# Denominators of the softmax from 32 rows ahead of v, and a range test of them for the bound on scores

## The chip, the cores and the metric

The kernel runs on one core of one Trainium2 chip. The metric is the device time of one execution in microseconds (us). Engines are named as in the profile: PE multiplies matrices, DVE, ACT and POOL work on vectors, SP issues most of the DMAs.

## The reference

Two layers on x of 8 images, 512 channels and 32 x 32 = 1024 positions, all in float32:

```python
# layer 0: attention over the positions, 8 heads of 64 channels
q, k, v = conv1x1(x, Wq, bq), conv1x1(x, Wk, bk), conv1x1(x, Wv, bv)
attn = softmax(einsum('bhdn,bhdm->bhnm', q, k) * 64 ** -0.5, axis=-1)
x = x + conv1x1(einsum('bhnm,bhdm->bhdn', attn, v).reshape(B, C, H, W), Wp, bp)
# layer 1: non-local block with 256 inner channels, then batch norm
theta, phi, g = (conv1x1(x, w, b).reshape(b, 256, n) for ...)
f = einsum('bcn,bdn->bcd', theta, phi) / n
z = conv1x1(einsum('bcd,bdn->bcn', f, g), W_w, W_b) + x
out = (z - mean) * rsqrt(var + 1e-5) * gamma + beta    # over batch and positions
```

## The kernel before

**Work of one image.** The kernel goes through the images b one by one: attention of b, then q, v and k of image b + 1, then the projection of b, its theta and phi, and the rest of the non-local block. The z of the last three images is finished late, in `last_z`, which also takes the batch norm's statistics, normalises and writes the output.

**Products.** Each 1x1 convolution is a product of 2 x 2 blocks, made by `seven` (L263) with seven block products in place of eight (Strassen's way, in Winograd's form); for q, k and the projection of most images some of the seven are again split so, by `nested` (L245). The sums of weight blocks that this needs are made once, on DVE (`weight_sums` L103, `keep_inner` L163), and kept in DRAM; `load_w` (L124) brings a kept set, up to 2.4 MB, back into a pool of two places. A set is issued on SP's queue when the product that used its place is done. The block products land in PSUM banks, of which there are four; ACT or DVE moves or adds them to the result (`first`, `add`), and a bank is used again when its reader is done. In v (`values` L408) the order of block products is 11, s1t1, s2t2, s4, s3t3, 12, t4, with eight matmuls (called units here, numbered from 0) each; the adds of v are at L418.

**Attention** (L436). For each pair of heads p and half of the queries h, PE makes scores for eight blocks of 128 keys (L462), ACT takes the exponential without a shift (L465), and DVE adds the eight results to `acc` (L469, L471), so that what is left for the denominator is a sum over 128 rows for each of two heads. `spread` (L503) brings each `acc` to `fold`: `together` (L498) writes the first quarter of its rows by a DMA of SP and adds the other three by accumulating DMAs of POOL, to 32 rows. When four are there, a second `together` (L524) adds the two halves of every pair of rows to 16.

**Denominators and normalisation.** `all_denominators` (L526) sums over the 16 rows by two matmuls with a matrix of ones and zeros (`folds8`), 64 columns wide, takes the reciprocal (L534, 128 x 512), writes 16 rows of it to DRAM (`den_d`, 32 KB, L536) and `rows_of` (L553) reads them back four times, each read spread over 64 partitions (`r`, 512 KB each, in 8 KB per partition, L558). `products` (L567) multiplies o by r in four DVE operations (L571). In the loop, `norm` does all but the products after v's block product 1 (that is, on PE between units 15 and 16), and the products follow v's block product 5. The last image has its own way (`denominators` L540), 128 x 512 at a time for half of the heads.

**Bound on the scores.** Because there is no shift, the kernel tests that the exponentials can't overflow: `peak_of` (L396) takes the largest |q| and |k| of every channel (64 reductions on DVE), `bound_scores` (L421) multiplies them, sums over the channels of a head by a small matmul with `heads`, compares with a bound, and multiplies q by the 0 or 1 that results (on POOL, L429). At the end of the program the smallest gate is counted by a matmul, read into a register, and the other program, `shifted`, is run if a test failed.

**What sets the order.** `pe`, `dve` and `sp` keep the instructions that are passed to them in the order of the program on PE, DVE and SP. All matmuls are pinned so; of the DVE's work, v's adds, the products o<-o,r, most of q's adds and data sums are, k's adds are not. The other instructions are placed by a scheduler when the kernel is built. SP issues DMAs in its order, and each waits at the head of its queue for what it needs. The `fold` pool has one place, used by `fold` and by `r` in turn.

## Time and profile before

| | us |
|---|---|
| three runs | 2145.25, 2145.33, 2148.92 |
| median | 2145.33 |
| span of the profiled execution | 2143.6 |
| period of one image (343.55 to 606.52) | 262.97 |
| PE busy in it | 262.85 |
| matmul of 512 columns, 128 x 128 | about 0.43 each |
| matmul of 256 columns, 128 x 128 | about 0.22 each |
| w_WkT load of 2368 KB, from issue to landing (median) | 8.8 |
| den_d store of 32 KB | 1.8 |
| r loads, 512 KB each (median) | 6.9 |
| last matmul | 2123.1 |

The profile is one execution. Its span runs from the first to the last instruction; the profiled execution's own time lies outside the page, and the median of the runs is 1.7 us above this span. Busy times of an engine are sums of its instructions; matmuls overlap at their edges by about 0.17 us, so a group's time is a little longer than the step to the next group. In a timeline each line is the start, the duration, the engine, the line of the kernel, the operation with what it writes and reads, the shape and the number of instructions; brackets give the idle time ahead of it and what ended it. SPq is SP's DMA queue: the duration there is that of issuing, not of the transfer.

### The profile page before, as it was taken

The numbers are of one execution on the slowest core, as the hardware profiler recorded it, in microseconds if no ns is written. First come the engines' busy times: TensorE is split into PE (matmuls) and PEld (weight loads), VectorE is DVE, ScalarE is ACT, GpSimd is POOL, SyncE is SP. The second block draws the span as 40 slices with busy tenths as digits, with TensorE's granted clock in tenths as the row PEclk, the third lists the DMA queues.
The fourth block names the chain that finished last, engine by engine and source line by source line (L and its number), as shares of the span: only waits on it lengthen the run. The fifth ranks groups of instructions, "written<-read, shape, count | busy, mean of one in ns | idle before, by whom it ended". The sixth has DMA issues, their size and how long they took to land.

```text
span 2143.6 us, 30444 instructions
## 1 busy us (share of the span) xinstructions
PE 2119.6 (99%) x12654; PEld 1123.3 (52%) x12654; DVE 1448.4 (68%) x1795; ACT 742.8 (35%) x848; POOL 193.2 (9%) x242
## 2 busy tenths in 40 slices
PE   9999999999999999999999999999999999999996
PEld 4534664356733567335673366633666347743462
DVE  6467667667676676766667667676675676756736
ACT  1464104641046310463105621066212652056106
POOL 0111000110001100011001100011000110011000
PEclk9999999999999999999999999999999999999998
DMA  6433443334143331433323342233434235122758
GB/s 242 137 46 58 136 166 127 49 71 129 73 131 49 79 116 73 133 50 83 109 102 109 48 100 99 97 107 50 108 132 161 42 45 139 52 60 39 227 197 341
DMA packets 53969, 231.05 MB, mean 108 GB/s; under 512 B 9792, under 2 KB 16192, under 8 KB 46272
## 3 DMA queue, kind: packets, MB, share of 16 engines
q1 hardware_dynamic: 42144, 199.26, 27.5%
q0 software_dynamic: 10192, 28.46, 11.0%
q8 instruction: 101, 1.65, 0.3%
q10 hardware_dynamic: 1488, 1.32, 0.2%
q14 instruction: 44, 0.36, 0.1%
HBM read 141.84 MB, written 46.27 MB: 88 GB/s over the span
## 4 chain that ended last, share of the span: by engine, by line
PE 96%; ACT 1%; DVE 1%; DMA 1%; issue 0%; SPq 0%; ACTq 0%; DVEq 0%
PE ps L462 21%; PE po L488 21%; PE pv L300 9%; PE ptp L300 9%; PE pp L300 7%; PE pk L300 6%; PE pq L300 5%; PE pg L300 4%; PE pk_in_s L255 3%; PE pq_in_s L255 3%; PE pz L300 2%; PE pf L658 2%; PE pp_in_s L255 2%; PE pwf L713 1%; ACT z L830 1%; PE pf L674 1%
## 5 line engine op out<-in xcount | busy, mean ns | idle before, releaser
L465 ACT ACTIVATE e<-ps 128x1024 f32<-128x1024 f32 x512 | 522.6, 1024 | 431.1 <-PE ps L462 425.6
L471 DVE TENSOR_TENSOR acc<-acc,e 128x1024 f32<-128x1024 f32 x384 | 470.0, 1224 | 143.7 <-ACT e L465 140.3
L462 PE MATMUL ps<-q,k 64*64 64x512 f32 x4096 | 529.4, 589 | 0.0
L488 PE MATMUL po<-e,v 64*64 64x512 f32 x4096 | 528.7, 589 | 0.0
L488 PEld LDWEIGHTS po<-e,v 64*64 64x64 f32 x4096 | 156.6, 133 | 282.9 <-issue 275.4
L462 PEld LDWEIGHTS ps<-q,k 64*64 64x64 f32 x4096 | 155.5, 133 | 283.8 <-issue 274.8
L501 POOL DMA_DIRECT2D fold<-acc x189 | 147.1, 779 | 978.9 <-DMA fold<-acc 576.6
L701 ACT ACTIVATE g<-pg,gb 128x512 f32<-128x512 f32 x31 | 21.3, 687 | 475.4 <-PE pg L300 475.3
L469 DVE TENSOR_TENSOR acc<-e,e 128x1024 f32<-128x1024 f32 x64 | 78.3, 1224 | 136.6 <-ACT e L465 136.6
L300 PE MATMUL pv<-w_WvT,t_x 128*128 128x256 f32 x512 | 116.4, 381 | 0.0
L300 PE MATMUL ptp<-w_tp,t_x 128*128 128x256 f32 x512 | 114.4, 379 | 0.0
L417 ACT COPY v<-pv 128x1024 f32<-128x1024 f32 x32 | 32.4, 1012 | 213.9 <-PE pv L300 213.9
L300 PEld LDWEIGHTS pv<-w_WvT,t_x 128*128 128x128 f32 x512 | 96.6, 190 | 18.5 <-issue 5.7
L300 PEld LDWEIGHTS ptp<-w_tp,t_x 128*128 128x128 f32 x512 | 97.3, 190 | 13.2
L300 PE MATMUL pq<-t_x,w_WqT 128*128 128x512 f32 x200 | 100.1, 592 | 0.8 <-DVE t_x L842 0.8
L300 PE MATMUL pp<-t_o,w_WpT 128*128 128x512 f32 x208 | 100.8, 592 | 0.0
L300 PE MATMUL pk<-t_x,w_WkT 128*128 128x512 f32 x200 | 100.0, 592 | 0.0
L429 POOL TENSOR_SCALAR q<-q,gates 128x1024 f32<-128x1024 f32 x32 | 35.1, 1109 | 718.4 <-DVE gates L427 718.4
L300 PE MATMUL ptp<-w_tp,x 128*128 128x256 f32 x384 | 87.4, 381 | 0.0
L300 PE MATMUL pv<-w_WvT,x 128*128 128x256 f32 x384 | 86.8, 379 | 0.0
L324 DVE TENSOR_TENSOR q<-q,pq_in_s 128x256 f32<-128x256 f32 x119 | 48.6, 420 | 51.1 <-PE pq_in_s L255 38.4
L324 DVE TENSOR_TENSOR k<-k,pk_in_s 128x256 f32<-128x256 f32 x119 | 47.9, 420 | 48.6 <-PE pk_in_s L255 36.0
(195 smaller groups left out, 2348.6 us busy)
## 6 DMA issues: line engine op xcount, KB each, us to landing
fold<-acc POOLq DMA_DIRECT2D x189, 128.0 KB, 3.1
w_WqT<-kept_WqT SPq DMA_DIRECT2D x7, 2368.0 KB, 8.8
w_WkT<-kept_WkT SPq DMA_DIRECT2D x7, 2368.0 KB, 8.8
r<-den_d SPq DMA_DIRECT2D x32, 512.0 KB, 6.9
x<-in_x_dram SPq DMA_DIRECT2D x30, 512.0 KB, 5.7
w_WpT<-kept_WpT SPq DMA_DIRECT2D x6, 2176.0 KB, 8.3
w_WvT<-kept_WvT SPq DMA_DIRECT2D x7, 1792.0 KB, 7.2
w_tp<-kept_tp SPq DMA_DIRECT2D x7, 1792.0 KB, 7.3
```

The costliest lines, as they stand in the source:

```text
L255: pe(nc.tensor.matmul(ps, a[wi], d[di], start=s not in begun, stop=True, skip_group_check=True))
L300: pe(nc.tensor.matmul(to_ps, lhsT(k), rhs(k), start=(s, at) not in begun, stop=(k == nk - 1), skip_group_check=True))
L324: pin(nc.vector.tensor_tensor(at, at, ps if len(ps.shape) == 3 else ps.unsqueeze(1), ALU.add))
L417: seven(f"pv_{b}", w, data, True, lambda q, ps: nc.scalar.copy(at(q), as_v(ps)), lambda q, ps: dve(nc.vector.tensor_tensor(at(q), at(q), a ...
L429: nc.gpsimd.tensor_scalar(q[:, p, :], q[:, p, :], gate[:, p:p + 1], 1.0, ALU.mult, ALU.mult)
L462: pe(nc.tensor.matmul(ps[c * P // 2:(c + 1) * P // 2, j, :], k[r, p, keys], q[r, p, h * 512:(h + 1) * 512], start=True, stop=True, skip_gr ...
L465: nc.scalar.activation(e, ps, AF.Exp, scale=SCALE)
L469: nc.vector.tensor_tensor(accs[u], es[u, 0], e, ALU.add)
L471: ins = nc.vector.tensor_tensor(accs[u], accs[u], e, ALU.add)
L488: pe(nc.tensor.matmul(ps[j * D:(j + 1) * D, r, :], v[keys, m, (2 * p + j) * D:(2 * p + j + 1) * D], e[keys, j, :], start=(m == 0), stop=(m ...
L501: nc.gpsimd.dma_start(to, part_of, accum_op=ALU.add)
L658: pe(nc.tensor.matmul(to, theta[l][:, i, :], phi[r][:, i, :], start=(i == 0), stop=(i == NB // 2 - 1), skip_group_check=True))
```

## The change

Four things are changed.

1. The test of the scores' bound goes: `peak_of`, `bound_scores`, the gates. In its place the reciprocals themselves are tested to lie between 1e-20 and 1e20: nine small loads bring them from DRAM into `dens` (128 x 512), and at the end two DVE operations compare, four transposes on PE and one reduction on DVE bring the result to one number per partition, which is counted as before.
2. The second folding goes. The denominators are summed from 32 rows by eight matmuls, 32 columns wide and 256 long, in four column tiles with two accumulating into each; the reciprocal is 128 x 256, `den_d` is [32, 256], and `r` is read in two pieces of 4 KB per partition, where it was one of 8 KB.
3. `den` moves from v to q's unit 14 (of 16), in a bank that q has finished with, and the four products o<-o,r from after v's block product 5 to v's units 32, 35, 38 and 41, each by itself. The reciprocal is pinned.
4. For image 0 the sums of WkT are pinned and come ahead of the inner sums and the store of WqT; the adds of every k are pinned.

Some code comes with it that these sizes do not use (`positions_out` in `nested`). In the order that is built, den_d, the four r and `dens` stand behind the load of w_WkT on SP's queue; before, they stood behind it as well, but were issued after v's block product 1.

```diff
-    def bound_scores(b, q, k, peak_q, peak_k):
-
-        nc.vector.tensor_tensor(peak_q, peak_q, peak_k, ALU.mult)
-        ps = next_bank(f"bound_{b}")[:, 0, :]
-        pe(nc.tensor.matmul(ps[:, :CC], heads, peak_q, start=True, stop=True))
...
-            if i == 3 and not make_f:
-                two = t[:, g, :].rearrange("(r s) n -> s r n", s=2)
-                together(t[g * D:(g + 1) * D, 2, :], [two[0], two[1]])
...
-            t, ps = t[:, 2, :], ps[:, 0, :]
-            columns(ps, folds8, lambda j: t[:, j * 512:(j + 1) * 512])
-            ri = t[:, :512]
-            nc.vector.reciprocal(ri, ps)
-            d = dram2.tile([16, 512], F32, tag="den", name=f"den_d_{b}")
-            nc.sync.dma_start(d, ri.rearrange("(a s) n -> a s n", a=16)[:, 0, :])
-            d = d.rearrange("(j g i) n -> g j (i n)", j=2, g=2)
-            return d[0], d[1]
+            ps, of = ps[:, 0, :256], P // 4
+            for g in range(2):
+                for i in range(4):
+                    pe(nc.tensor.matmul(ps[i * of:(i + 1) * of, :], folds4[:, g * of:(g + 1) * of],
+                                        t[:, g, i * 256:(i + 1) * 256], start=(g == 0), stop=(g == 1),
+                                        skip_group_check=True))
+            ri = t[:, 2, :256]
+            dve(nc.vector.reciprocal(ri, ps))
+            d = dram.tile([of, 256], F32, tag=f"den{b}", name=f"den_d_{b}")
+            nc.sync.dma_start(d, ri.rearrange("(x s) n -> x s n", s=4)[:, 0, :])
+            own.append((dens[:, b * 64:(b + 1) * 64], d.rearrange("x (y n) -> (x y) n", y=4)))
+            return d.rearrange("(j h g i) m -> g j h i m", j=2, h=2, g=2)
...
+                to = rows[g][j * D:(j + 1) * D, :]
+                if len(d.shape) == 4:
+                    to = to.rearrange("q (h n) -> q h n", h=2)
+                    sp(nc.sync.dma_start(to, d[j].rearrange("h i m -> h (i m)").partition_broadcast(D)))
...
-    q, peak_q = heads_of(0, "q", weights("WqT", True), bq, data, early=True, by_chunk=True)
-    keep_inner("WqT", w_first)
-    load_w(nc.sync)
+    q = heads_of(0, "q", weights("WqT", True), bq, data, dve, early=True, by_chunk=True)
...
-    w = weights("WkT")
-    k, peak_k = heads_of(0, "k", w, bk, data)
+    w = weights("WkT", pin=dve)
+    keep_inner("WqT", w_first)
+    load_w(nc.sync)
+    k = heads_of(0, "k", w, bk, data, dve)
...
+                     14: lambda: nxt.update(products=normalize(denominators(bank(free[0], f"den_{b}"))))}
+            q = heads_of(b + 1, "q", weights("WqT"), bq, nxt["data"], dve, inner="WqT", fills=fills)
             load_w(nc.sync)
-            def norm():
-                nxt["products"] = normalize(denominators(next_bank(f"den_{b}")))
-
-            v = values(b + 1, weights("WvT"), nxt["data"], {1: norm, 2: lambda: [one() for one in later], 5: lambda: nxt["products"]()})
+            free[:] = [free[2], free[1], free[0], free[3]]
+            v = values(b + 1, weights("WvT"), nxt["data"],
+                       fills={unit: lambda i=i: nxt["products"][i]() for i, unit in enumerate((32, 35, 38, 41))})
...
+    for to, d in own:
+        nc.sync.dma_start(to, d)
     last_z()
...
+    nc.vector.tensor_scalar(sane, dens, 1.0 / SANE, 1.0, ALU.is_ge, ALU.mult)
+    nc.vector.scalar_tensor_tensor(sane, dens, SANE, sane, ALU.is_le, ALU.mult)
+    ps = next_bank("sane_t")[:, 0, :]
+    for i in range(512 // P):
+        pe(nc.tensor.transpose(ps[:, i * P:(i + 1) * P], sane[:, i * P:(i + 1) * P], ident))
+    nc.vector.tensor_reduce(good, ps, AX.X, ALU.min)
```

More of the change, by code (lines that the diff above doesn't have):

```diff
@@ L19 @@
 EPS = 1e-5
-BOUND = 60.0
+SANE = 1e20
 def attention_nonlocal_kernel(tc: tile.TileContext, a: dict, out: bass.AP):
@@ L140, in load_w, with weights @@
             dma.dma_start(to, quarter(name, m, k))
-    def weights(name, sums_done=False):
+    def weights(name, sums_done=False, pin=lambda ins: None):
         n, w = loaded.pop(0)
@@ L147, in weights @@
             if not sums_done:
-                weight_sums(w, corner[name])
+                weight_sums(w, corner[name], pin=pin)
             if name not in ("WqT", "WkT"):
@@ L168, in keep_inner @@
                                  (s4, a12, s2, ALU.subtract)):
-                nc.vector.tensor_tensor(to, l, r, op)
+                dve(nc.vector.tensor_tensor(to, l, r, op))
         wide = len(INNER[name]) * 3 * P
@@ L243, in unshifted, with nested @@
              15: ((0, "22", False), (0, "21", False))}
-    def nested(name, stage, w, data, tags, first, add):
+    def nested(name, stage, w, data, tags, first, add, positions_out=False):
         slots = [bank(tag, f"{name}_in_{tag}") for tag in tags]
@@ L254, in nested @@
                 ps = pair[s % 2 if s < 2 else 1][:, s // 2, n % 2 * 256:(n % 2 + 1) * 256]
-                pe(nc.tensor.matmul(ps, a[wi], d[di], start=s not in begun, stop=True, skip_group_check=True))
+                if positions_out:
+                    ps = ps.rearrange("p (i f) -> p i f", f=P)
+                    for i in range(2):
+                        pe(nc.tensor.matmul(ps[:, i, :], d[di][:, i * P:(i + 1) * P], a[wi], start=s not in begun and not i,
+                                            stop=True, skip_group_check=True))
+                else:
+                    pe(nc.tensor.matmul(ps, a[wi], d[di], start=s not in begun, stop=True, skip_group_check=True))
                 begun.add(s)
                 for to, is_first in reads:
+                    if positions_out:
+                        (first if is_first and begins else add)((q, int(to[0]) - 1, int(to[1]) - 1), ps)
+                        continue
                     c = rows(q).start + int(to[0]) - 1
@@ L275, in seven @@
             free[:] = [tags[1], tags[2], tags[3], tags[0]]
-            steps = nested(name, inner, w, data, tags[2:], first, add)
+            steps = nested(name, inner, w, data, tags[2:], first, add, positions_out)
         def read(reads, ps):
@@ L295, in seven @@
                          for m in range(half // P)]
-            work = [(*part, k) for part in (parts if m is None else parts[m:m + 1]) for k in range(nk)]
+            each = len(parts) // 2
+            work = [(*part, k) for part in (parts if m is None else parts[m * each:(m + 1) * each]) for k in range(nk)]
             if by_chunk and what in ("11", "s1t1"):
                 work.sort(key=lambda one: one[4])
-            for to_ps, at, lhsT, rhs, k in work:
+            for i, (to_ps, at, lhsT, rhs, k) in enumerate(work):
                 pe(nc.tensor.matmul(to_ps, lhsT(k), rhs(k), start=(s, at) not in begun, stop=(k == nk - 1),
@@ L302, in seven @@
                 begun.add((s, at))
+                if three and positions_out and not i % 2:
+                    continue
                 for ahead in (True, False):
@@ L328, in unshifted @@
     xt = xp.tile([P, CC, N], F32, tag="x", name="x_0")
-    heads = const.tile([P, P], F32, tag="heads", name="heads")
-    nc.vector.memset(heads, 0.0)
+    zeros = w3.tile([P, N], F32, tag="acc", name="zeros")[:, :P]
+    nc.vector.memset(zeros, 0.0)
     _, w_first = weights_tile("WqT", C // 2)
@@ L344, in unshifted @@
     for i in range(WARM):
-        pe(nc.tensor.matmul(ps[:, :P], heads, heads, start=True, stop=True))
+        pe(nc.tensor.matmul(ps[:, :P], zeros, zeros, start=True, stop=True))
     bq, bk = load_col("bq", nc.scalar), load_col("bk", nc.scalar)
@@ L357, in unshifted @@
         nc.vector.memset(folds[i * P // 4:(i + 1) * P // 4, i * D // 4:(i + 1) * D // 4], 1.0)
-    folds8 = const.tile([P, D], F32, tag="folds8", name="folds8")
-    nc.gpsimd.memset(folds8, 0.0)
-    nc.gpsimd.affine_select(out=folds8, in_=folds8, compare_op=ALU.is_gt, fill=1.0, base=1 - P // 8,
-                            pattern=[[-P // 8, 8], [0, D // 8]], channel_multiplier=1)
-    nc.gpsimd.affine_select(out=folds8, in_=folds8, compare_op=ALU.is_ge, fill=0.0, base=0,
-                            pattern=[[-P // 8, 8], [0, D // 8]], channel_multiplier=1)
-    for j in range(2):
-        nc.vector.memset(heads[j * D:(j + 1) * D, j * D:(j + 1) * D], 1.0)
+    folds4 = const.tile([P, D], F32, tag="folds4", name="folds4")
+    nc.vector.memset(folds4, 0.0)
+    for i in range(4):
+        for at in (i * 4, P // 4 + 16 + i * 4):
+            nc.vector.memset(folds4[i * P // 4:(i + 1) * P // 4, at:at + 4], 1.0)
     mv = const.tile([P, CC, 2], F32, tag="mv", name="mv")
-    gates = const.tile([P, B * NPAIR], F32, tag="gates", name="gates")
+    dens = const.tile([P, B * HEADS * N // P], F32, tag="dens", name="dens")
     ngamma = const.tile([P, CC], F32, tag="ngamma", name="ngamma")
@@ L374, in halves, with heads_of @@
         return t.rearrange("p (h n) -> p h n", h=NH)
-    def heads_of(b, what, w, bias, data, pin=lambda ins: None, later=None, **how):
+    def heads_of(b, what, w, bias, data, pin=lambda ins: None, **how):
         t = mats.tile([P, CC, N], F32, tag=what, name=f"{what}_{b}")
-        peak = small.tile([P, CC], F32, tag=f"peak_{what}", name=f"peak_{what}_{b}")
         def first(q, ps):
@@ L394, in heads_of, with values @@
         seven(f"p{what}_{b}", w, data, False, first, add_to(t, pin), **how)
-        def peak_of(c):
-            ins = nc.vector.tensor_reduce(peak[:, c:c + 1], t[:, c, :], AX.X, ALU.max, apply_absolute_value=True)
-            if b == 0 or later is not None:
-                dve(ins)
-        for c in range(CC):
-            if later is None:
-                peak_of(c)
-            else:
-                later.append(lambda c=c: peak_of(c))
-        return t, peak
-    def values(b, w, data, between=None):
+        return t
+    def values(b, w, data, **how):
         v = mats.tile([P, NB, C], F32, tag="v", name=f"v_{b}")
         def at(q):
+            if isinstance(q, tuple):
+                q, o, n = q
+                n, o = (int(q[1]) - 1) * NB // 2 + n * 2, (int(q[0]) - 1) * C // 2 + o * P
+                return v[:, n:n + 2, o:o + P]
             return v[:, (int(q[1]) - 1) * NB // 2:int(q[1]) * NB // 2, (int(q[0]) - 1) * C // 2:int(q[0]) * C // 2]
         def as_v(ps):
-            return ps.rearrange("p h (i f) -> p (h i) f", f=C // 2)
+            return ps if ps.shape[2] == P else ps.rearrange("p h (i f) -> p (h i) f", f=C // 2)
         seven(f"pv_{b}", w, data, True, lambda q, ps: nc.scalar.copy(at(q), as_v(ps)),
-              lambda q, ps: dve(nc.vector.tensor_tensor(at(q), at(q), as_v(ps), ALU.add)), between)
+              lambda q, ps: dve(nc.vector.tensor_tensor(at(q), at(q), as_v(ps), ALU.add)), **how)
         return v
-    def bound_scores(b, q, k, peak_q, peak_k):
-        nc.vector.tensor_tensor(peak_q, peak_q, peak_k, ALU.mult)
-        ps = next_bank(f"bound_{b}")[:, 0, :]
-        pe(nc.tensor.matmul(ps[:, :CC], heads, peak_q, start=True, stop=True))
-        gate = gates[:, b * NPAIR:(b + 1) * NPAIR]
-        nc.vector.tensor_scalar(gate, ps[:, :CC], BOUND / SCALE, 1.0, ALU.is_le, ALU.mult)
-        for p in range(NPAIR):
-            nc.gpsimd.tensor_scalar(q[:, p, :], q[:, p, :], gate[:, p:p + 1], 1.0, ALU.mult, ALU.mult)
     def columns(ps, lhsT, rhs):
@@ L530, in all_denominators @@
                 bias_product(t[:, 3, :], ps[:, 1, :CC])
-            t, ps = t[:, 2, :], ps[:, 0, :]
-            columns(ps, folds8, lambda j: t[:, j * 512:(j + 1) * 512])
-            ri = t[:, :512]
-            nc.vector.reciprocal(ri, ps)
-            d = dram2.tile([16, 512], F32, tag="den", name=f"den_d_{b}")
-            nc.sync.dma_start(d, ri.rearrange("(a s) n -> a s n", a=16)[:, 0, :])
-            d = d.rearrange("(j g i) n -> g j (i n)", j=2, g=2)
-            return d[0], d[1]
+            ps, of = ps[:, 0, :256], P // 4
+            for g in range(2):
+                for i in range(4):
+                    pe(nc.tensor.matmul(ps[i * of:(i + 1) * of, :], folds4[:, g * of:(g + 1) * of],
[7 more added lines that the diff above has]
+            return d.rearrange("(j h g i) m -> g j h i m", j=2, h=2, g=2)
         def denominators(g, ps):
@@ L548, in denominators @@
                 rows_of(0, first_den)
-            d = dram2.tile([8, 512], F32, tag=f"den{g}", name=f"den_d_{b}_{g}")
+            d = dram2.tile([8, 512], F32, tag=f"last{g}", name=f"den_d_{b}_{g}")
             nc.sync.dma_start(d, ri.rearrange("(a s) n -> a s n", a=8)[:, 0, :])
+            own.append((dens[:, b * 64 + g * 32:b * 64 + (g + 1) * 32], d.rearrange("a (x n) -> (a x) n", x=16)))
             return d.rearrange("(j i) n -> j (i n)", j=2)
@@ L557, in rows_of @@
             for j in range(2):
-                sp(nc.sync.dma_start(rows[g][j * D:(j + 1) * D, :], d[j].partition_broadcast(D)))
+                to = rows[g][j * D:(j + 1) * D, :]
+                if len(d.shape) == 4:
+                    to = to.rearrange("q (h n) -> q h n", h=2)
+                    sp(nc.sync.dma_start(to, d[j].rearrange("h i m -> h (i m)").partition_broadcast(D)))
+                else:
+                    sp(nc.sync.dma_start(to, d[j].partition_broadcast(D)))
         def normalize(d):
@@ L565, in normalize, with product @@
             r = rows["all"]
-            def products():
-                for g in range(2):
-                    for h in range(NH):
-                        at = o["o"][:, 2 * g:2 * g + 2, h * 512:(h + 1) * 512]
-                        dve(nc.vector.tensor_tensor(at, at, r[:, 4 * g + h:4 * g + 4:2, :], ALU.mult))
-            return products
+            def product(g, h):
+                at = o["o"][:, 2 * g:2 * g + 2, h * 512:(h + 1) * 512]
+                of = r[:, 4 * g + h:4 * g + 4:2, :]
+                if not make_f:
+                    of = r[:, 4 * g:4 * g + 4, :].rearrange("q (k a) (c m) -> q (a c) k m", k=2, c=2)[:, h::2]
+                    at = at.rearrange("q p (k m) -> q p k m", k=2)
+                dve(nc.vector.tensor_tensor(at, at, of, ALU.mult))
+            return [lambda g=g, h=h: product(g, h) for g in range(2) for h in range(NH)]
         for i in range(len(steps) + LAG):
@@ L750, in nonlocal_ @@
             nc.sync.dma_start(spill[b][:, oc, :], xt[:, oc, :])
-    late, z = {}, {}
+    late, z, own = {}, {}, []
     def put_away(b):
@@ L851, in unshifted @@
     nc.sync.dma_start(tpb[:, 1, 0, :], a["phi_b"].partition_broadcast(P))
-    w = weights("WkT")
-    k, peak_k = heads_of(0, "k", w, bk, data)
+    w = weights("WkT", pin=dve)
+    keep_inner("WqT", w_first)
+    load_w(nc.sync)
+    k = heads_of(0, "k", w, bk, data, dve)
     keep_inner("WkT", w)
     load_w(nc.sync)
-    v = values(0, weights("WvT"), data, {3: lambda: bound_scores(0, q, k, peak_q, peak_k)})
+    w = weights("WvT")
+    v = values(0, w, data)
     load_w(nc.sync)
@@ L883, in unshifted @@
         if not last:
-            later, of_22, of_t4 = [], [], []
+            of_22, of_t4 = [], []
             fills = {4: lambda: (of_22.extend(inner_parts(nxt["data"], "22", dve)),
@@ L888, in unshifted @@
                      6: lambda: (of_t4[0](), of_t4[1]()), 7: lambda: (of_t4[2](), of_t4[3]()),
-                     8: lambda: (of_22[0](), of_22[1]()), 9: lambda: (of_22[2](), of_22[3]())}
-            q, peak_q = heads_of(b + 1, "q", weights("WqT"), bq, nxt["data"], dve, inner="WqT",
-                                 later=later, fills=fills)
+                     8: lambda: (of_22[0](), of_22[1]()), 9: lambda: (of_22[2](), of_22[3]()),
+                     14: lambda: nxt.update(products=normalize(denominators(bank(free[0], f"den_{b}"))))}
+            q = heads_of(b + 1, "q", weights("WqT"), bq, nxt["data"], dve, inner="WqT", fills=fills)
             load_w(nc.sync)
-            def norm():
-                nxt["products"] = normalize(denominators(next_bank(f"den_{b}")))
-            v = values(b + 1, weights("WvT"), nxt["data"], {1: norm, 2: lambda: [one() for one in later], 5: lambda: nxt["products"]()})
+            free[:] = [free[2], free[1], free[0], free[3]]
+            v = values(b + 1, weights("WvT"), nxt["data"],
+                       fills={unit: lambda i=i: nxt["products"][i]() for i, unit in enumerate((32, 35, 38, 41))})
             load_w(nc.sync)
@@ L908, in unshifted @@
                     fills[unit] = lambda which=which: weight_sums(w_p, corner["WpT"], which, dve)
-            later_k = []
-            k, peak_k = heads_of(b + 1, "k", weights("WkT"), bk, nxt["data"], later=later_k, inner="WkT",
-                                 fills=fills)
+            k = heads_of(b + 1, "k", weights("WkT"), bk, nxt["data"], dve, inner="WkT", fills=fills)
             if b:
@@ L919, in unshifted @@
             between = {4: late_unit(b - 1, 0, sums_now=False)}
-            normalize(nxt["d"])()
+            for one in normalize(nxt["d"]):
+                one()
             load_w(nc.sync)
@@ L940, in unshifted @@
         tp = theta_phi(b, weights("tp"), data, {} if last else
-                       {5: lambda: b < B - 2 and of_theta.append(f_sums(b, tps[0], 0)), 1: lambda: [one() for one in later_k[:2]], 2: lambda: [one() for one in later_k[2:]],
-                        4: lambda: bound_scores(b + 1, q, k, peak_q, peak_k)})
+                       {5: lambda: b < B - 2 and of_theta.append(f_sums(b, tps[0], 0))})
         load_w(nc.sync)
@@ L962, in unshifted @@
         xt = nxt.get("x")
+    for to, d in own:
+        nc.sync.dma_start(to, d)
     last_z()
-    good = const.tile([P, 1], F32, tag="good", name="good")
-    nc.vector.tensor_reduce(good, gates, AX.X, ALU.min)
+    good, (sane, ident) = const.tile([P, 1], F32, tag="good", name="good"), (block("sane")[:, i, :] for i in range(2))
+    ident = ident[:, :P]
+    make_identity(nc, ident)
+    nc.vector.tensor_scalar(sane, dens, 1.0 / SANE, 1.0, ALU.is_ge, ALU.mult)
[4 more added lines that the diff above has]
+    nc.vector.tensor_reduce(good, ps, AX.X, ALU.min)
     ps = next_bank("count")[:, 0, :]
```

## The prediction

> **What bounds the kernel now.** I read the totals first, then the chain that ended last, then the table by stage for one period (from image 1 to image 2).

> ```profile
> PE 2119.6 (99%) x12654; PEld 1123.3 (52%) x12654; DVE 1448.4 (68%) x1795; ACT 742.8 (35%) x848; POOL 193.2 (9%) x242
> ...
> PE 96%; ACT 1%; DVE 1%; DMA 1%; issue 0%; SPq 0%; ACTq 0%; DVEq 0%
> ```

> PE is busy 99% of the span and makes 96% of the chain. In the period 343.55 to 606.52, 262.97 us long, its busy time is 262.85. So inside an image two things alone move the end: work put on or taken off PE, and a new moment in which PE has to wait. DVE (68%) and POOL (9%) work counts only where it makes PE late. The base is the profiled execution: span 2143.6 us; the median of the runs, 2145.33, is 1.7 above it, and I add those 1.7 at the end.

> The place that matters is v of the next image. On the timeline of before:

> ```profile
> 476.42 3.62 PE L300 MATMUL pv<-w_WvT,x 128*128 128x256 f32 x16
> ...
> 483.42 1.08 PE L434 MATMUL den<-fold,folds 128*64 128x512 f32 x4
> ```
> ```profile
> 476.61 0.33 SPq L134 DMA_DIRECT2D w_WkT<-kept_WkT  x1
> 487.93 0.50 SPq L536 DMA_DIRECT2D den_d<-fold  x1
> 489.85 2.40 SPq L558 DMA_DIRECT2D r<-den_d  x4
> ```
> ```profile
> 484.55 3.36 DVE L534 RECIPROCAL fold<-den 128x512 f32<-128x512 f32 x1 [5.25 <-PE den L434]
> ...
> 495.09 1.22 DVE L418 TENSOR_TENSOR v<-v,pv 128x1024 f32<-128x1024 f32 x1 [1.61 <-PE pv L300]
> 498.55 1.22 DVE L418 TENSOR_TENSOR v<-v,pv 128x1024 f32<-128x1024 f32 x1 [2.23 <-PE pv L300]
> 499.68 2.35 DVE L571 TENSOR_TENSOR o<-o,r 128x1024 f32<-128x1024 f32 x2
> 502.35 1.23 DVE L571 TENSOR_TENSOR o<-o,r 128x1024 f32<-128x1024 f32 x1 [0.31 <-DMA r<-den_d]
> ```

> Columns: start, duration, engine, line, operation; in brackets the idle time before it and who ended it. The reader is to see the order: the 2.4 MB load of w_WkT goes out at 476.61 and is over before den_d is issued at 487.93; the four r loads follow; the products o*=r (L571) stand behind v's adds, and the third of them already waits 0.31 us for r. No matmul waits for any of it.

> **Part by part.**

> Bound on scores. PE loses one pair of matmuls per image (theta_phi, `bound`). The chain goes from ptp at 284.99 for 17.27 us to ptp at 302.38: 302.38 - 302.26 = 0.12 between them, and with the disturbed pipeline about 0.22. Eight of them: -1.8 us. The 64 peaks on DVE (73.7 us) and the gate products on POOL (35.1 us) lie beside PE and bring nothing.

> Denominators. Before: 4 records of 512 columns, two at a time (two 64-column tiles), 1.01 us on the chain, about 1.2 with the v products beside them slowed. After: 16 records of 256 columns. 256-column records of full tiles follow each other in 0.216 us; four at a time (as the 64x64 score matmuls do, 8 records of 512 columns in 0.86 us) they are 4 x 0.216 = 0.86 us plus the same edges, 1.2 us. Change 0. Bounds: edges gone, -0.34 x 7 = -2.4; one after another, 16 x 0.216 = 3.5, which is +2.6 x 7 = +18. I take 0, the score row being the nearest. The second folding that goes (28 DMAs of SP and POOL) ran beside PE; the first folding's last DMA is issued at 465.12 and, at the page's 3.1 us, lands at 468.3. den now stands at q's unit 14, about 475.1: 7 us of slack, no wait.

> Start. PE waited 0.84 us at 15.96 for t_x on DVE, which had waited 1.86 for w_WkT (L169). The new order removes that: -0.84. But the store of WqT moves behind k's sums, so w_WvT lands some 1.7 us later, its sums push k's adds, and k's last product may wait about 1.0. Together +0.2, bounds -0.8 to +2.

> End. The test adds DVE work in an idle stretch and one reduction ahead of the last statistics, about 0.65 us. From 2097 to 2139 the DMA engines are at share 1.00 with the output, so I count 0, bound +0.7. The nine small `dens` loads, 128 KB in all a few KB at a time, are behind r on the queue: 0.

> The normalisation is where I expect a price. den moves ahead of v, so v starts on PE at P = 476.42 + 1.2 = 477.6; the products move from after v's product 5 to units 32, 35, 38 and 41. On DVE the order becomes: add of s4, three products, add of s3t3 (v<-pv_0), fourth product, last add. The add of s3t3 frees the bank that t4 writes (unit 48). So **PE now waits at t4 for the third product, and this for r.** Step by step, from P:
> - w_WkT is still issued when q lets its slot go, P+0.2, and stands on SP's queue now ahead of den_d (issued about P+0.6). Its page median is 8.8 us: it lands at P+9.0.
> - den_d is alone a 1.8 us transfer. Behind 2.4 MB of the same queue I put it at P+9.2. The trace shows such small loads behind large ones: a_WkT (256 KB, 4.5 us), then bvc of 2 KB, 4.1 us.
> - The four r loads go out from P+9.3. At 1278.78 those of another image took, from the first issue, until +12.0 for the last. In the stretch 491.2:500.4 the queue was full with them:

> ```profile
> q1 hardware_dynamic: 295, 2.02, 100.5%
> ```
>   that is 2.02 MB in 9.2 us, 220 GB/s. So the last r lands at P+21.3.
> - Third product and add of s3t3: 2.36 us (two of 1.2, as L571's pair shows) and 0.1: PE may go on at P+23.8.
> - PE is there at 6 products x 3.45 us = P+20.7. **Stall 3.1 us, in 7 images: +21.8.**

> Bounds: if den_d overtakes w_WkT, both then share the engines; r's bytes still come after most of w_WkT's at 220 GB/s, and 0.7 is left. r is now read in 4 KB pieces, two for each partition. w_WkT's own, in 479.2:484.2, moved at 402 GB/s; if r does so too, the 2.02 MB take some 4.4 us less and the stall is 0. If the smaller pieces cost instead (the 128 KB loads of tpb, in 1 KB pieces, take 3.6), 5.3 to 6.5. I take 3.1: same destination, bytes and source as the row of before.

> What then falls out behind: a stall shifts everything of the image by the same amount, k's first adds find DVE done with the fourth product within 2.4 us of t4's start; nothing is late next.

> On the queue: the row of bvc (2 KB, 4.1 us, issued just behind 256 KB) agrees with a queue that works in order. [...]

> On the clock: in before it falls only once PE has stopped (last matmul 2123.1; granted clock 1.00 until 2127, 0.81 in the next us, then 0.50). [...]

> Sum: -1.8 + 0.2 + 0 + 21.8 + 0 = +20.2; 2143.6 + 20.2 = 2163.8 of span, **2165.5** with the 1.7.

> **Rivals.**
> - B, r comes in time: then only -1.8 + 0.2 are left, 2143.7, with den's and the start's lower ends down to 2145.3 - 1.8 - 0.8 - 2.4 = 2140.3. This is the other side of my forecast: one mechanism, r's transfer, at L558; it decides when the last r lands ahead of P+18.2 (20.7 - 2.46). For it: the 402 GB/s of long rows, and that den is issued over 10 us earlier than before. Against: 220 GB/s at equal bytes, and w_WkT ahead of it.
> - C, r is slower in halved pieces, and PE waits 5.3 to 6.5 us: 37 to 46 more, 2181 to 2190, above that if PE's clock falls in the gap. For it: the tpb row. Against: 4 KB is far from 1 KB.
> - D, the change doesn't do what it says: four column tiles run one after another, +18 on top of A, 2183. Against: the score matmuls run four at a time.

> **How the numbers follow.** A (stall of 2 to 5 us, 2158 to 2179): 0.64. B: 0.19, of it 0.03 below 2141. C: 0.13. D: 0.04. 0.2% is 4.3 us, about what a measurement of this kernel tells from no change. Slower: A, C, D = 0.81; within: 0.16; faster: 0.03. Range 2143 to 2186: it leaves out C's and B's far ends, some 0.2. A's own range is 2158 to 2179.

> **What would show it.** In the profile after: an idle time of about 3 us on PE ahead of v's last product, with DVE as releaser, seven times; on DVE the L571 successor waiting for r; den_d landing some 9 us after issue, not 1.8; four r landing up to 21 us after v's start. den's group on the chain at 1 us (step right) or 3.5 (D); no `bound` rows; no wait of PE at 16 us; the last output's DMA as busy as before. The forecast is wrong if the last r lands before P+18, above all if its rate is near 400 GB/s.

## The result and the profile after

The changed kernel takes 2174.95 us (four runs, 2169.64 to 2180.28), against 2145.43 before on the same chip: ratio 1.0135, interval 1.012 to 1.0149. Forecast was 2165.5, slower, with a range to 2186. The profiled execution has a span of 2172.2, 28.6 us above that of before; its own time is 2174.09.

The totals of the page, and its chain by engine:

```profile
PE 2128.9 (98%) x12726; PEld 1127.7 (52%) x12726; DVE 1362.5 (63%) x1724; ACT 742.7 (34%) x848; POOL 145.5 (7%) x195
...
PE 90%; DMA 6%; DVE 2%; SPq 1%; issue 0%; ACT 0%; DVEq 0%
```

DVE has 86 us less to do and POOL 48, and it is slower: what counted is that DMA now makes 6% of the chain. The table of PE's waits (time in all, times, longest) has at its head a row that before had not:

```profile
PE pv L310 <- DVE v L420: 20.5, 7, 3.7
```

The place, in the same image as in the prediction. P, the start of v on PE, is now 481.96. PE, then SP's queue, then DVE:

```profile
481.96 3.62 PE L310 MATMUL pv<-w_WvT,x 128*128 128x256 f32 x16
...
499.23 3.62 PE L310 MATMUL pv<-w_WvT,x 128*128 128x256 f32 x16
506.10 5.41 PE L310 MATMUL pv<-w_WvT,t_x 128*128 128x256 f32 x16 [3.26 <-DVE v L420]
```
```profile
482.15 0.33 SPq L134 DMA_DIRECT2D w_WkT<-kept_WkT  x1
482.58 0.49 SPq L529 DMA_DIRECT2D den_d<-fold  x1
491.06 2.59 SPq L555 DMA_DIRECT2D r<-den_d  x4
```
```profile
499.46 2.36 DVE L572 TENSOR_TENSOR o<-o,r 128x1024 f32<-128x1024 f32 x2 [2.19 <-DMA r<-den_d]
503.69 1.23 DVE L572 TENSOR_TENSOR o<-o,r 128x1024 f32<-128x1024 f32 x1 [1.87 <-DMA r<-den_d]
504.83 1.21 DVE L420 TENSOR_TENSOR v<-v,pv 128x1024 f32<-128x1024 f32 x1
```

Read from below: the add at 504.83 frees t4's bank; the third product at 503.69 stands ahead of it and waited for r; r went out at 491.06 only, since den_d, issued at 482.58, landed 8.3 us later. The chain of waits goes just this way, from the reciprocal to t4:

```profile
480.70 1.76 DVE fold L527
482.46 0.12 DVE q L336
482.58 8.34 DMA den_d<-fold
...
493.04 10.56 DMA r<-den_d
...
503.69 1.23 DVE o L572
504.92 1.14 DVE v L420
506.06 0.04 issue
506.10 5.41 PE pv L310 x16
```

The last line holds what I had not put into the sum: t4's 16 matmuls take 5.41 us where the same 16 took 3.62. By stretches of 1 us (PE busy, PEld, DVE, ACT, POOL, then the granted clock, DMA share, GB/s):

```profile
505.00:506.00 1.00, 0.00 (x0) 0.00 (x0) 1.00 (x2) 0.00 (x0) 0.00 (x0) 1.00 0.00 0
506.00:507.00 1.00, 0.90 (x4) 0.82 (x5) 1.00 (x2) 0.00 (x0) 0.00 (x0) 1.00 0.00 0
507.00:508.00 1.00, 1.00 (x5) 0.84 (x4) 1.00 (x2) 0.00 (x0) 0.00 (x0) 0.63 0.00 0
508.00:509.00 1.00, 1.00 (x3) 0.75 (x3) 0.32 (x1) 0.00 (x0) 0.00 (x0) 0.50 0.00 0
509.00:510.00 1.00, 1.00 (x4) 0.81 (x3) 0.00 (x0) 0.00 (x0) 0.00 (x0) 0.50 0.00 0
510.00:511.00 1.00, 1.00 (x5) 0.82 (x4) 0.00 (x0) 0.00 (x0) 0.00 (x0) 0.67 0.00 0
```

The clock is at 1.00 when PE resumes and falls to half a little later, for about 3.4 us.

Where the 28.6 us came from, by the start of each stage on PE in both traces: the start, up to the first v, -0.4; `bound` gone, -0.22 in each of 8 images, -1.8; v of seven images +29.9 (without den, which adds to q what it takes out of v: 1.20, in image 1 2.3); k and single edges some +1.0; the end -0.1. Of the 29.9, about 21.6 is the stall: t4 starts 2.7 to 3.9 us after it was due, P+20.72 (the starts of the matmuls on both sides of the gap lie 2.9 to 4.1 us apart; the 20.5 of the table counts from the modelled end of the matmul before). The other 8.3 is t4 taking longer: 8.0 at half clock, in four of the seven images (two with 1.8 us, one with 1.7, one with 2.7), and 0.1 in each of the other three.

### The profile page after: what moved, and what is told of

It is laid out like the page before. It is cut to its first block, busy times and chain, and to the rows that moved or that the text cites. A ratio compares the mean times of both kernels' runs of the same rounds, so it can differ in the third digit from the quotient of the medians.

```text
span 2172.2 us, 30403 instructions
## 1 busy us (share of the span) xinstructions
PE 2128.9 (98%) x12726; PEld 1127.7 (52%) x12726; DVE 1362.5 (63%) x1724; ACT 742.7 (34%) x848; POOL 145.5 (7%) x195
## 4 chain that ended last, share of the span: by engine, by line
PE 90%; DMA 6%; DVE 2%; SPq 1%; issue 0%; ACT 0%; DVEq 0%
PE ps L454 20%; PE po L480 20%; PE ptp L310 9%; PE pp L310 7%; PE pk L310 5%; PE pq L310 5%; PE pg L310 4%; DMA r<-den_d 3%; PE pk_in_s L261 3%; PE pq_in_s L261 3%; DMA den_d<-fold 3%; PE pv L310 3%; PE pz L310 2%; PE pz L790 2%; PE pf L659 2%; PE pp_in_s L261 2%
## 5 line engine op out<-in xcount | busy, mean ns | idle before, releaser
L702 ACT ACTIVATE g<-pg,gb 128x512 f32<-128x512 f32 x31 | 21.3, 687 | 474.3 <-PE pg L310 474.2
L310 PE MATMUL pv<-w_WvT,t_x 128*128 128x256 f32 x512 | 122.7, 398 | 20.5 <-DVE v L420 20.5
L310 PEld LDWEIGHTS pv<-w_WvT,t_x 128*128 128x128 f32 x512 | 102.0, 200 | 38.4 <-DVE v L420 23.3
L420 DVE TENSOR_TENSOR v<-v,pv 128x1024 f32<-128x1024 f32 x24 | 29.2, 1218 | 94.4 <-PE pv L310 94.4
L310 PEld LDWEIGHTS ptp<-w_tp,x 128*128 128x128 f32 x384 | 73.0, 190 | 13.3 <-issue 3.8
```

The source lines that it names most:

```text
L310: pe(nc.tensor.matmul(to_ps, lhsT(k), rhs(k), start=(s, at) not in begun, stop=(k == nk - 1), skip_group_check=True))
```

## The experiments

Theory: PE waits because the add of s3t3 stands behind the third product, which needs r; r is late because den_d's 32 KB are queued behind w_WkT; the clock falls because PE idled. Rivals: the wait is DVE's work, not r; den_d and r are slow by their small pieces; the fall of the clock has another reason.

**Products behind the add** (`e1_products_behind`).

```diff
-                       fills={unit: ... for i, unit in enumerate((32, 35, 38, 41))})
+                       fills={unit: ... for i, unit in enumerate((40, 41, 42, 43))})
```

> The changed kernel with the four products o<-o,r at v's units 40 to 43, all behind the add of s3t3, in place of 32, 35, 38 and 41. Theory (PE waits at t4 because that add stands behind the third product, which waits for r): the wait of 20.5 us at t4 goes, and with it the 7.7 us that t4's matmuls took longer behind it; span about 2144.0, time about 2146, not to be told from before. den_d and r land as late as in the changed kernel. Rival 1 (the wait is the work of DVE, not r): with the same DVE work around t4 some 5 to 10 us stay. Rival 2 (t4 is slow for another reason than PE's idling): 7 to 8 us stay.

Measured: 2144.24 us, ratio 0.9991 (0.9982 to 1.0), span 2142.9. On DVE the add comes first, and the products still wait for r, beside PE:

```profile
494.17 1.22 DVE L420 TENSOR_TENSOR v<-v,pv 128x1024 f32<-128x1024 f32 x1 [2.16 <-PE pv L310]
495.31 2.35 DVE L572 TENSOR_TENSOR o<-o,r 128x1024 f32<-128x1024 f32 x2
498.40 2.36 DVE L572 TENSOR_TENSOR o<-o,r 128x1024 f32<-128x1024 f32 x2 [0.74 <-DMA r<-den_d]
```

den_d still takes 8.0 us. So lateness of r costs next to nothing by itself; all 29.3 us hang on the products' place ahead of an add. Once, in one image, the projection waits 0.8 us for the last product.

**Two products ahead** (`e7_two_ahead`): units 32, 35, 41, 42.

> The changed kernel with two products ahead of the add of s3t3 (units 32 and 35) and two behind it (41 and 42). The first two need only r's first two loads. In the changed kernel they end at P+19.9; the add then ends at P+21.0, and PE is due at P+20.7. Theory: 0.3 to 0.5 us of waiting in each of 7 images, 2 to 3.5 in all, and no fall of the clock; span about 2145.5. Rival (the place of the add behind any product costs the wait, not the third one's r): 10 us or more stay.

Measured: 2145.31 us, ratio 0.9999 (0.9989 to 1.0009), span 2143.5; PE's wait at t4:

```profile
PE pv L310 <- DVE v L420: 0.8, 2, 0.5
```

Less than expected: r's second load lands at P+16.2 to P+17.8 in the images that show it, so in most of them the two products and the add are done ahead of P+20.7. It is not a product ahead of the add that costs, but the third, which needs r's last load.

**Four products ahead** (`e5_four_ahead`): units 32, 35, 37, 38.

> The changed kernel with all four products ahead of the add of s3t3 (units 32, 35, 37, 38). Theory: PE waits one more DVE operation, 1.15 us, in each of 7 images, about 28.6 in all, and as every idle time is then 3.9 us or more, the clock falls in all seven images, 1.7 to 2.7 us each (16.8 by the middle of what the changed kernel shows): span about 2189, time about 2191. Rival (the fall of the clock has nothing to do with the length of the idle time): +8 alone, span about 2180.

Measured: 2189.49 us, ratio 1.0196 (1.0181 to 1.0212), span 2187.8. The wait is 26.4 us in seven images, 2.2 below the expectation (3.4 to 4.2 us each), and t4 runs partly at half clock in all seven (5.4 to 6.7 us for its 16 matmuls).

**w_WkT behind r** (`e2_wk_behind_r`).

```diff
-            if len(queue) == 1:
+            if len(queue) == 1 or name == "WkT":
                 sp(ins)
```

> The changed kernel with the load of w_WkT pinned on SP's queue behind the four r loads; products as in the changed kernel. Theory (den_d takes 8.2 us because it is queued behind 2.4 MB): den_d lands 1.8 us after its issue, the last r at about P+14.5 (P is the start of v on PE), the wait at t4 is 0, w_WkT lands by about P+20 and k (P+24.2) doesn't wait; span about 2144, time about 2146. Rival (den_d and r are slow because of their own small pieces, not the order): den_d still takes 5 us or more, and 5 to 20 us of waiting stay. Second rival (w_WkT is late next): PE waits for it at k's start, 1 to 4 us for each of 7 images.

Measured: 2143.58 us, ratio 0.999 (0.9981 to 0.9999), span 2141.8, the shortest of all, if only by 0.1 us. SP's queue, where the load of w_WkT now is third:

```profile
477.69 0.49 SPq L529 DMA_DIRECT2D den_d<-fold  x1
479.50 2.59 SPq L555 DMA_DIRECT2D r<-den_d  x4
482.19 0.79 SPq L134 DMA_DIRECT2D w_WkT<-kept_WkT  x1
```

Here P is 477.16. den_d lands in 1.7 us, the last r at P+14.5 to P+16.4, and w_WkT at P+20 to P+22, before k needs it at P+24.2. No wait at t4, none at k. This shows that w_WkT's place ahead of den_d and r is the cause; it does not tell whether by the queue or by the engines behind it.

**The same, on other queues** (`e3_pool_queue`: den_d and r issued by POOL; `e9_den_on_act`: den_d alone issued by ACT).

```diff
-            nc.sync.dma_start(d, ri.rearrange("(x s) n -> x s n", s=4)[:, 0, :])
+            nc.gpsimd.dma_start(d, ri.rearrange("(x s) n -> x s n", s=4)[:, 0, :])
...
-                    sp(nc.sync.dma_start(to, d[j].rearrange("h i m -> h (i m)").partition_broadcast(D)))
+                    sp(nc.gpsimd.dma_start(to, d[j].rearrange("h i m -> h (i m)").partition_broadcast(D)))
```

> The changed kernel with den_d and the four r issued on POOL's queue in place of SP's; w_WkT stays where it is, so it still moves at the same time. Theory (it is the order within SP's queue): den_d lands 2 to 4.5 us after its issue (POOL's small folding DMAs take 3.1), r goes out by P+5.5 and the last lands by about P+17; the wait at t4 is 0 to 0.5 us per image, span 2142 to 2146. Rival (the DMA engines are shared, whatever the queue): den_d takes 6 us or more, the last r lands at P+19 or later, and 10 to 20 us of waiting stay, with falls of the clock, span 2155 to 2172.

Measured: 2160.15 us, ratio 1.0072 (1.0055 to 1.0089), span 2157.4, the rival's. den_d takes 6.2 us on POOL's queue, and the last r lands at P+20 (P is 478.17):

```profile
478.96 0.58 POOL L529 DMA_DIRECT2D den_d<-fold  x1 [12.53 <-DVE q L336]
485.80 2.35 POOL L555 DMA_DIRECT2D r<-den_d  x4 [6.25 <-PE pv L310]
```

So my theory, that it is the order within SP's queue, falls: most of den_d's delay stays on another queue. In `e9_den_on_act` the first line of the edit has `nc.scalar` and r stays on SP's queue.

> The changed kernel with den_d alone issued on ACT's queue; w_WkT and the four r stay on SP's. On POOL's queue den_d took 6.2 us, against 8.2 on SP's and 1.8 with nothing ahead of it, which left two readings. Reading 1 (a DMA engine serves the 2.4 MB that stand ahead first, whatever queue the 32 KB came by): den_d takes 5 to 7 us here too, r is issued at about P+7 and goes on behind w_WkT, its last lands at P+18.5 to P+19, and 0.2 to 1 us per image are left of the wait, span 2145 to 2150. Reading 2 (queues share the engines in turn, and the 6.2 was POOL's own way of issuing): den_d takes 2 to 4 us, r is issued by P+4.5; its bytes still move at 220 GB/s.

Measured: 2160.69 us, ratio 1.0076 (1.0059 to 1.0093), span 2158.2. den_d takes 7.0 us on ACT's queue as well: reading 1. The rest of it was wrong in size: the last r lands at P+20, not P+18.5 to P+19, and 12.5 us of waiting stay. The first r, issued at P+7.5 to P+8.0 in place of P+8.8 to P+9.5, lands 5 us after its issue as before, and from w_WkT's landing at P+9 to the last r there are 11 us: r gained about what den_d gained, and no more. In one image of this run, and in one of `e3_pool_queue`, the clock fell too, 1.8 us each. So with den_d on another queue 13.8 to 14.6 us of the 28.6 stay.

**den_d, w_WkT, r** (`e10_den_wk_r`): all three pinned on SP's queue, and r's loads moved behind the load of w_WkT.

```diff
-            if len(queue) == 1:
+            if len(queue) == 1 or name == "WkT":
...
-            nc.sync.dma_start(d, ri.rearrange("(x s) n -> x s n", s=4)[:, 0, :])
+            sp(nc.sync.dma_start(d, ri.rearrange("(x s) n -> x s n", s=4)[:, 0, :]))
...
-                     14: lambda: nxt.update(products=normalize(denominators(bank(free[0], f"den_{b}"))))}
+                     14: lambda: nxt.update(d=denominators(bank(free[0], f"den_{b}")))}
...
             load_w(nc.sync)
+            nxt["products"] = normalize(nxt["d"])
```

> The changed kernel with SP's queue in the order den_d, w_WkT, r (pinned), where it was w_WkT, den_d, r, and the best run had den_d, r, w_WkT. Theory (what is late is den_d and then r's 9.2 us of transfer, one after the other, behind w_WkT): den_d takes 1.8 us; r, issued at about P+2.5, moves behind w_WkT (landing at about P+9.4) and its last lands at P+18.5 to P+19.5; third product and add end at P+21 to P+22, so 0.3 to 1.3 us per image stay of the wait, 2 to 9 us in all, with no fall of the clock: span 2145 to 2151. Rival (r shares the engines with w_WkT in turn): the last r lands by P+16, no wait at t4, span 2142.

Measured: 2155.81 us, ratio 1.005 (1.0034 to 1.0067), span 2153.7, above the 2145 to 2151 expected. The mechanism is the theory's:

```profile
479.37 0.49 SPq L529 DMA_DIRECT2D den_d<-fold  x1
479.95 0.53 SPq L134 DMA_DIRECT2D w_WkT<-kept_WkT  x1
481.19 2.61 SPq L555 DMA_DIRECT2D r<-den_d  x4
```

den_d lands in 1.7 us, r waits behind w_WkT (landing at P+10.5 here, P is 478.84) and its last lands at P+19.4 to P+20.2; PE waits 8.8 us in all, at the upper end of the 2 to 9, and the clock stays up. With w_WkT behind it, den_d needs 1.7 us of its own; with w_WkT ahead, 8.2. But r's bytes behind w_WkT are late too, so den_d's overtaking alone brings 1.7 us per image (the gaps fall from 21.6 to 9.9 us in all), and r's the other 1.4.

**Work in the gap** (`e4_busy_gap`, `e6_busy_three`). Matmuls that nobody reads, ahead of t4, so that PE does not idle:

```diff
+            def busy():
+                ps = bank(free[0], f"busy_{b}")[:, 0, :]
+                for i in range(6):
+                    pe(nc.tensor.matmul(ps, w_v[:, 0, 0, :P], nxt["x"][:, 0, :512], start=True, stop=True))
...
-            v = values(b + 1, weights("WvT"), nxt["data"],
+            v = values(b + 1, w_v, nxt["data"], between={5: busy},
```

> The changed kernel with six more matmuls of 512 columns (2.6 us) on PE ahead of t4, into a bank that nobody reads: they do nothing for the output and lie in the time in which PE waits. Theory (t4's matmuls run at half the granted clock in some images because PE idled for about 3 us): the rest of the gap is 0.3 to 1.5 us, no matmul of t4 takes 0.43 us, PE resumes at the same P+23.4 to P+24.6, and the span is 7.7 us shorter, about 2164.5; the runs lie closer together than the 10.6 us of the changed kernel. Rival (the clock falls for another reason, such as the DMA load): the span stays at about 2172.

Measured: 2179.87 us, ratio 1.016 (1.0146 to 1.0174), span 2177.9, longer than the changed kernel. The size was mine: a matmul of 512 columns makes two records, and six took 5.2 us, all of the gap and 2 us more.

```profile
502.64 5.31 PE L902 MATMUL busy<-x,w_WvT 128*128 128x512 f32 x12
507.79 3.62 PE L310 MATMUL pv<-w_WvT,t_x 128*128 128x256 f32 x16
```

But t4 is back at 3.62 us in all seven images, and the runs lie within 1.5 us of each other. With three of them (`e6_busy_three`):

> As the run with six idle-time matmuls, with three: there each made two records of 0.43 us, so six took 5.2 us where 2.6 were meant. Three take 2.6 us, inside the 2.9 to 4.1 us of the changed kernel's gap. Theory (the clock falls because PE idles for 3 us or more): what is left of the gap is 0.3 to 1.5 us, every t4 matmul takes 0.22 us, PE resumes at P+23.4 to P+24.6 as in the changed kernel; span 2172.2 - 7.7 = 2164.5, and the runs lie within 5 us of each other. Rival (the clock falls for another reason): span about 2172, runs 10 us apart.

Measured: 2164.96 us, ratio 1.0091 (1.0074 to 1.0107), span 2163.6, and runs from 2164.67 to 2165.53. PE resumes between P+23.4 and P+25.2 (one image with a late r), no t4 matmul takes more than 0.22 us apart from edges. The fall of the clock follows from PE's idling: with the gap filled, none of the fourteen images of the two runs shows one (in the image with the late r the granted clock here is 1.00 from 505 to 509). Of the 8.6 us of span that this run saves, 7.6 are t4's own time and the rest small differences elsewhere; the spread of the changed kernel's runs went with them.

**The bound alone** (`e8_before_no_bound`): the kernel before without peaks, bound matmuls and gates on q.

> The kernel before without the bound on scores: no peaks, no bound matmuls, no gates on q (the gates are set to 1, so the test is left out); all else as before. Step of the prediction: -0.22 us in each of 8 images on PE and nothing from DVE's 73.7 us and POOL's 35.1: span 2141.8, time 0.08% less than before. Rival (the freed DVE and POOL time brings something): 2140 or less.

Measured: 2143.8 us, ratio 0.9994 (0.9984 to 1.0003), span 2141.9. By the stages' starts, -0.22 us in each image and nothing else: some 109 us of work off DVE and POOL brought nothing.

## Why the prediction was right, and where it was not

The forecast had the place, the sign and the wait; the time was 9.5 us above it, inside the range, and a term that the sum held at nothing made up most of that. By its steps:

- **The stall**, 3.1 us in 7 images, 21.8: measured 21.6 by the gaps. den_d's landing was put at P+9.2, measured P+8.7 to P+9.3; the last r at P+21.3, measured P+21.1 to P+22.1; PE's resuming at P+23.8, measured P+23.4 to P+24.6. r moved at 215 GB/s in 4 KB pieces, near the 220 of the 8 KB pieces:

```profile
q1 hardware_dynamic: 469, 1.72, 98.5%
```
  (the 8 us from 493.5 in the changed kernel: packets, MB, share; 1.72 MB in 8 us). So neither the 402 GB/s of rival B nor the slower pieces of C came.
- **Why den_d waits** was half right. The queue's order is not needed for it: on ACT's and POOL's queues it still took 7.0 and 6.2 us. What decides is that 2.4 MB were given to the DMA engines ahead of it: with the same two loads the other way round on SP's queue it took 1.7 us. That the landing came out at P+9 does not show the queue's order to be the reason.
- **The clock** is the term that failed. The sum held nothing for it. Four of the seven stalls had a fall: those of 3.85, 3.42, 3.06 and 2.89 us, the last two no longer than the 3.1 of the forecast, while one of 2.93 had none. Together the falls cost some 8 us, which is nearly all of the difference between forecast and profile (28.6 against 20.2).
- **The start**: forecast +0.2, measured -0.4. The wait at 16 us went as worked out, but k's last product did not come late by 1.0: k's add of 48.63 ended at 49.84, ahead of PE, and k's stage came out only 0.17 longer.
- **den**, 0: measured 1.20 into q and 1.20 out of v (2.3 in image 1), 0. Four column tiles do run at once: 16 records take 1.04 us on the chain, so D is out.

```profile
479.63 1.04 PE den L523 x16
```
- **The bound**, -1.8: measured -1.8, in the change and alone.
- **The end**, 0: measured -0.1. The reduction of the test stands ahead of the last statistics and takes 0.68 us, 0.60 of it on the chain; the output's DMAs are at a share of 0.98 from 2125 to 2167, which would hide it, but no run takes the test alone out. The nine loads of `dens` carry 256 KB (seven of 32 KB, two of 16), not the 128 of the forecast; no matmul waits for them.
- **Rival B** (r in time, 2143.7) is what `e2_wk_behind_r` makes of this change: span 2141.8 and time 2143.58. Its deciding point, r by P+18.2, holds there (P+14.5 to P+16.4) and is missed in `e10_den_wk_r` (P+19.4 to P+20.2) and `e9_den_on_act` (P+20), which wait. (At 402 GB/s the 2.02 MB would have taken 4.2 us less, not 4.4; nothing hangs on it.)

## What to carry to other kernels

Before an operation is moved up in an engine's order, ask what stands behind it: here four multiplications had all the time they wanted, and cost 29 us because one of them, waiting for a load, stood ahead of the add that frees a PSUM bank. A small transfer on which a chain hangs goes out ahead of a large one that has time, and another queue is no full substitute for that: here it left 13.8 to 14.6 of 28.6 us. And an idle time of 3 us on PE cost up to 5 in all here, since in four of seven images the clock fell to 0.50 after it, for 3.4 or 6.8 us; so price the stall with the clock's fall, or fill it.

## What the runs showed of the hardware

```profile
773.49:776.90 3.41, 3.21 (x8) 2.58 (x9) 2.42 (x3) 0.00 (x0) 0.00 (x0) 0.50 0.00 0
1572.21:1579.04 6.83, 5.34 (x13) 4.26 (x14) 3.71 (x4) 0.00 (x0) 0.00 (x0) 0.50 0.00 0
```

The first is one step long, the second two. In `e5_four_ahead` all seven returns lie on a grid of the same step. Take the 28 stalls of four profiles (the changed kernel, e5, e9 and e3), each counted from when t4 was due and divided where a step of its profile's grid begins. Every one with at most 2.01 us of idling within a single step is without a fall, and every one with 2.04 or more has one (in the changed kernel's own seven at most 1.74 and at least 2.26); by the profile's idle times, which start at the modelled end of the last matmul, the two sides are 1.85 and 1.91. The seven stalls of e10 (at most 1.91 in a step, counted from when t4 was due) had no fall and fit. So the length of the gap alone does not tell: one of 2.1 us fell (in e9, lying wholly in one step) and one of 2.9 did not (in the changed kernel, 1.43 and 1.50 in two steps). The same 13 falls tell how long half clock lasts: one step in seven of them, where PE was idle for at most 0.20 us after the fall, and two steps in the other six, where it was idle for 0.73 to 1.56 us. The changed kernel's runs lie 10.6 us apart; only one was profiled, so whether the falls make that difference is not shown.

**32 KB waited behind 2.4 MB on each queue that was tried.** They took 8.2 us on the same queue, 7.0 on ACT's and 6.2 on POOL's, and 1.7 with nothing ahead. Why they waited on the other two as well stays open.

**r's rate** was 215 to 220 GB/s in both piece sizes (windows above), against about 400 for w_WkT just ahead of it (402 in the window of the prediction). In the other orders, too, one load of 512 KB landed a median of 2.3 to 2.5 us after the one before it, 213 to 228 GB/s. What holds it there was not tried; each read of r goes out to 64 partitions, which w_WkT's does not.
